# A conditioned four-stage residual kernel on one core: the first five periods from one written list, W1 laid out by 4p+c

## The chip, the cores and the metric

The kernel runs on one core of a Trainium2 chip. The metric is the device time of one execution in microseconds (us); lower is better. The engines are named as in the profile: PE (TensorE, matrix products; PEld its weight loads), DVE (VectorE), ACT (ScalarE), POOL (GpSimd) and SP (SyncE, which here only issues DMAs).

## What is computed

There are 128 samples x of 128 positions and 512 features. Four stages follow each other, each adding its result to x. The reference, cut to what matters:

```python
# stage 0, mask chosen by the sample's prompt type
s = einsum(tanh(x @ W0 + b0), v)                       # one score a position
p = softmax(where(mask[pt], s[:, None, :], -1e30))
x = x + (p @ x) / mask_count
# stage 1, weights chosen by the sample's language, 10 languages
a = relu(x @ W1[lang] + b1[lang]) @ W2[lang] + b2[lang]
x = x + layernorm(x + a) * gamma[lang] + beta[lang]
# stage 2, y = x as a 128 x 512 plane, reflecting edges
x = x + zX * lap_x(y) + zY * lap_y(y) + zR * y * (1 - y)
# stage 3, weights chosen by the sample's category, 64 categories
x = x + x @ W3[cat] + b3[cat]
```

W0 and W1[lang] are 512 x 128, W2[lang] is 128 x 512, W3[cat] is 512 x 512. All of it is float32.

## The kernel before

One sample is one tile: 128 positions on the partitions, 512 features along them. Stages 0 and 1 both begin with a product of x with a 512 x 128 matrix. These two products are taken together (`first_products`): x is turned so that features stand on the partitions, in four chunks of 128, and multiplied with W1[lang] and W0 side by side, held in `w10[b % 2]`. x + p @ x / count is then one product with p' = p / count + identity (`pooled`), and the adapter's second product is added to the same PSUM bank (`adapter`).

The order of all instructions is written out by hand. The list `plan` holds 46 parts, each with an offset: in period i the part (n, f) works on sample i + n. The stages of one sample so lie in different periods: first products for sample i + 1, pooling for i - 1, adapter for i - 2, the plane stage for i - 3 and the projection with W3 for i - 4. The main loop runs i from -2 to B + 4. The engines run their own instructions in that order and wait for each other by semaphores. Samples are loaded four periods ahead (`FIRST = 4`).

How x is turned. For samples 0 and 1 (`EARLY_X = 2`) `rejoin` turns x with four PE transposes and one ACT copy out of PSUM. For all others `halves` (an ACT copy, L247) splits the floats into two planes of 16-bit halves, `x_transpose` turns them with a transposing DMA on SP (L254), and `rejoin` (an ACT copy, L269) joins the halves.

Where W1 comes from. The table `w1_tab` holds W1 of all ten languages in SBUF, with b1 in one more column of each row (`W = D + 1`). `first_weights` copies the sample's row into `w10` (an ACT copy). For the first seven samples (`EARLY_W = 7`) `early_weights` loads W1[lang] straight from memory into `w10`, since the table is not there yet. Feature c*128 + p stands on partition p in chunk c; a chunk's rows are pieces of 512 bytes in memory.

What else the start must do. b2, gamma and beta of ten languages each (30 rows) have to be spread over all partitions. They are cut into three bfloat16 parts, and one PE product per row with a selecting column (`spread`, L230) writes the row into PSUM on all partitions; ACT or DVE copies it to its table (L233). The first four periods (`EARLY = 4`) run a changed copy of `plan` (`early_plan`), and the dictionary `once` hangs the spreading, the loading of `w1_tab` (`load_w1`, L118) and the factors of the plane stage onto parts of certain periods. `counts` (the number of allowed positions) and `neg_v` (-v) are made on DVE. b0 and v are broadcast by DMAs on ACT's queue, the ids, W2's table and the z factors come by SP.

Other lines that matter: L266 the PE transposes of x and L267 their copy (`rejoin`), L292 `first_products` (tile zh), L303 `hidden_bias`, L339 `scores` (sc), L369 and L374 `mix_transpose` and `mix_copy` (pTp, pT), L379 and L381 `pooled` (pool, h), L395 `with_beta` (POOL), L403 `adapter`, L426 `deviation` (POOL), L462 and L465 `y_transpose` (tr_y, tr_e), L471 to L473 `planes`, L515 `category` (the 1 MB of W3[cat]), L530 `residual` (POOL adds the identity to W3's diagonal, at steps of four floats), L537 `project` (po).

Of the kernel before, what the change touches and what calls it, by code (L numbers as in the profile page):

```python
# [10 lines left out]
I32 = mybir.dt.int32  # L11
# [12 lines left out]
def kernel(  # L24
# [46 lines left out]

    xt, w3t, b3t = {}, {}, {}
    FIRST = 4

    EARLY_X, EARLY_W = 2, 7
    W = D + 1
# [8 lines left out]
    def language(engine, b):  # L85
        return engine.snap(index(engine, 1, b, L - 1) * W)
# [4 lines left out]
    def early_weights(b):  # L91
        lang = index(nc.sync, 1, b, L - 1)
        nc.sync.dma_start(
            w10[b % 2][:, 0, :, :], w1[ds(lang, 1)].rearrange("o (c p) a -> p (o c) a", p=P)
        )

    ids = const.tile([1, 3, B], I32, name="ids")
    nc.sync.dma_start(ids[:, 1, :], lang_ids.unsqueeze(0))
    load_x(0)
    nc.sync.dma_start(w10[0][:, 1, :, :], w0.rearrange("(c p) a -> p c a", p=P))  # L100
    load_x(1)
    early_weights(0)
    early_weights(1)
    load_x(2)


    w1_tab = const.tile([P, L * W], F32, name="w1_tab")
    w2_tab = const.tile([A, L * W], F32, name="w2_tab")
    b2_tab = const.tile([P, L * W], F32, name="b2_tab")
    beta_tab = const.tile([P, L * W], F32, name="beta_tab")  # L110
    gamma_tab = const.tile([P, L * W], F32, name="gamma_tab")
# [4 lines left out]
    def load_w1(languages):  # L116
        for l in languages:
            nc.sync.dma_start(  # L118
                rows(w1_tab)[:, l, :D].rearrange("p (c a) -> p c a", c=NC),
                w1[l].rearrange("(c p) a -> p c a", p=P),  # L120
            )
# [14 lines left out]
    b0_sb = const.tile([P, A], F32, name="b0_sb")  # L136
    v_sb = const.tile([P, A], F32, name="v_sb")
# [7 lines left out]
    for dst, src in ((b0_sb, b0), (v_sb, v0)):  # L145
        nc.scalar.dma_start(dst, src.rearrange("a o -> (a o)").partition_broadcast(P))
    nc.sync.dma_start(ids[:, 0, :], pt_ids.unsqueeze(0))
    nc.sync.dma_start(ids[:, 2, :], cat_ids.unsqueeze(0))
    nc.sync.dma_start(rows(w2_tab)[:, :, :D], w2.rearrange("l a h -> a l h"))
    load_x(3)  # L150
    for dst, src in ((zx, z_x), (zy, z_y), (zr, z_r)):
        nc.sync.dma_start(dst, src.partition_broadcast(P))
    nc.sync.dma_start(rows(w1_tab)[:, :, D:W], b1t.unsqueeze(2))
# [3 lines left out]
    nc.gpsimd.tensor_copy(w10[1][:, 1, :, :], w10[0][:, 1, :, :])  # L157
# [20 lines left out]
    for i, (cmp, mult, step) in enumerate(  # L178
        ((ALU.is_ge, -1, 1), (ALU.is_ge, 1, -1), (ALU.not_equal, 1, -1))
    ):  # L180
        nc.gpsimd.affine_select(
            out=masks[:, i * P : (i + 1) * P],
            in_=masks[:, i * P : (i + 1) * P],
            compare_op=cmp,
            fill=BIG,
            base=0,
            pattern=[[step, P]],
            channel_multiplier=mult,
        )

# [9 lines left out]
    def counts():  # L200

        nc.vector.tensor_copy(row, row_i)
        nc.vector.tensor_scalar(d_pre, row, 1.0 - (S - 1), None, ALU.add)
        nc.vector.tensor_scalar(d_post, row, -1.0, 1.0, ALU.mult, ALU.add)
        nc.vector.tensor_copy(ptf, pt_i)
        nc.vector.tensor_scalar(cnt, ptf, 0.0, d_pre, ALU.is_equal, ALU.mult)
        nc.vector.tensor_scalar(sel, ptf, 1.0, d_post, ALU.is_equal, ALU.mult)
        nc.vector.tensor_add(cnt, cnt, sel)
        nc.vector.tensor_scalar_add(cnt, cnt, float(S - 1))

    counts()
    neg_v = const.tile([P, A], F32, name="neg_v")
    nc.vector.tensor_scalar_mul(neg_v, v_sb, -1.0)

    def factors():

        nc.vector.tensor_add(cy, zx, zy)
        nc.vector.tensor_scalar(cy, cy, -2.0, 1.0, ALU.mult, ALU.add)
        nc.vector.tensor_add(cy, cy, zr)
        nc.vector.tensor_scalar_mul(nzr, zr, -1.0)  # L220


    to_spread = [(t, i * L + l, l) for i, t in enumerate((b2_tab, gamma_tab, beta_tab)) for l in range(L)]

    def spread(n):
        for i in range(n):
            table, r, l = to_spread.pop(0)
            pool, tag = (ps_big, "big") if r % 3 else (ps_out, "po")
            ps = pool.tile([S, D], F32, tag=tag, name=f"row_{r}")
            nc.tensor.matmul(  # L230
                ps, pick[:, r : r + 1].to_broadcast([3 * G, P]), parts, start=True, stop=True
            )
            (nc.scalar.copy if r % 2 else nc.vector.tensor_copy)(rows(table)[:, l, :D], ps)  # L233
# [7 lines left out]
    def halves(b):  # L241
# [5 lines left out]
        nc.scalar.copy(s["split"], xt[b].bitcast(U16).rearrange("s (d i) -> s i d", i=2))  # L247
# [12 lines left out]
    def rejoin(b):  # L260
        s = st[b]
        s["xT"] = two.tile([P, NC, S], F32, tag="xT", name=f"xT_{b}")
        if b < EARLY_X:
            ps = ps_tr.tile([P, NC, S], F32, tag="tr", name=f"tr_x_{b}")
            for c in range(NC):
                nc.tensor.transpose(ps[:, c, :], xt[b][:, c * P : (c + 1) * P], ident)  # L266
# [7 lines left out]
    def act_index(b):  # L274
        st[b]["act_at"] = language(nc.scalar, b)

    def first_weights(b):
        if b < EARLY_W:
            if b > 1:
                early_weights(b)  # L280
            return
        nc.scalar.copy(
            w10[b % 2][:, 0, :, :].rearrange("p c a -> p (c a)"),
            w1_tab[:, ds(st[b]["act_at"], D)],
        )

    def first_products(b):
# [3 lines left out]
        for c in range(NC):  # L291
            nc.tensor.matmul(  # L292
                s["zh"],
                s["xT"][:, c, :],
                w10[b % 2][:, :, c, :],
                start=(c == 0),
                stop=(c == NC - 1),
            )
# [84 lines left out]
    def pooled_copy(b):  # L383
# [3 lines left out]
            s["h1"], s["h1p"], AF.Relu, bias=w1_tab[:, ds(s["act_at"] + D, 1)]  # L387
# [152 lines left out]

    def finish(b):
        nc.vector.tensor_add(b3t[b], st[b]["po"], b3t[b])

    def store(b):
# [20 lines left out]
        (-4, lambda b: project(b, [0])),  # L565
# [9 lines left out]
        (-4, lambda b: project(b, [1, 2])),  # L575
        (-1, pe_index),
        (-4, lambda b: project(b, [3])),
# [21 lines left out]

    EARLY = 4  # L600
    early_plan = list(plan)
    for part, place in (
        ((1, rejoin), (0, hidden)),
        ((1, first_products), (1, rejoin)),
        ((2, act_index), (-1, category)),
        ((2, first_weights), (2, act_index)),
    ):
        early_plan.remove(part)
        early_plan.insert(early_plan.index(place) + 1, part)
    once = {  # L610
        (-1, rejoin): [(spread, 8)],
        (0, first_products): [(spread, 3)],
        (0, masked): [(spread, 3)],
        (0, shares): [(spread, 3)],
        (1, first_products): [(spread, 3)],
        (1, masked): [(spread, 4)],
        (1, shares): [(spread, 6), (factors,)],
        (1, load_x): [(load_w1, range(0, 4))],
        (2, load_x): [(load_w1, range(4, 8))],
        (3, load_x): [(load_w1, range(8, L))],  # L620
    }
    for i in range(-2, B + 5):
# [43 lines left out]
```

## Time and profile before

| what | us |
|---|---|
| median of 3 runs | 1091.52 |
| lowest and highest | 1088.99 and 1091.77 |
| the profiled execution, its own time | 1090.35 |
| its span, first to last instruction | 1088.4 |
| PE busy | 1052.8 |
| DVE busy | 923.1 |
| ACT busy | 808.6 |
| POOL busy | 731.2 |

The profile is of one execution, so durations read from it are to be set against its own 1090.35 us. The granted PE clock over the span is 0.990 of full. A row of busy time by group gives line, engine, operation, tiles and shape, then how often, the total and the mean. The chain of waits follows the work that ended last back to its start. HBM delivered 209.13 MB and took 33.55 MB, together 223 GB/s over the span.

### The profile page before, as it was taken

The page shows a single profiled execution, that of the slowest core. Times are in us where ns is not written, and L with a number is a line of the kernel's source. Part 1 is how long each engine was busy: PE and PEld are TensorE (multiplying, and loading weights), DVE is VectorE, ACT ScalarE, POOL GpSimd, SP SyncE. Part 2 cuts the span into 40 slices and gives each one's busy share as a digit, 9 for nine tenths or more (in the row PEclk, how much of TensorE's full clock was granted, in tenths as well). Part 3 has the DMA queues.
Part 4 walks back from the last instruction along what each step waited for, and adds up shares of the span by engine and source line. Part 5 has one row for each costly group of instructions (what it writes and reads, how often), then busy time and mean ns, then how long its engine had stood idle before and what let it go on. Part 6 is the DMA issues. An engine that isn't in the chain of part 4 may idle for free.

```text
span 1088.4 us, 18571 instructions
## 1 busy us (share of the span) xinstructions
PE 1052.8 (97%) x3878; PEld 638.7 (59%) x3878; DVE 923.1 (85%) x2215; ACT 808.6 (74%) x1928; POOL 731.2 (67%) x780
## 2 busy tenths in 40 slices
PE   4689999999999999999999999999999999999997
PEld 2356566665666656666666566666665666656653
DVE  4568888888888888888888888888888888888886
ACT  3467877778778777787777777877777778777762
POOL 1156776767767667677676776776767767767675
PEclk9789999999999999999999999999999999999999
DMA  7699999999999999999999999999999999999973
GB/s 216 170 284 278 255 260 265 265 266 260 250 275 258 266 257 261 265 248 272 268 259 272 245 259 268 253 264 269 261 261 266 255 271 251 275 249 252 272 221 116
DMA packets 219920, 276.93 MB, mean 254 GB/s; under 512 B 142978, under 2 KB 152965, under 8 KB 203427
## 3 DMA queue, kind: packets, MB, share of 16 engines
q1 hardware_dynamic: 219318, 275.50, 97.5%
q8 instruction: 33, 0.54, 0.2%
q14 instruction: 77, 0.62, 0.2%
q10 hardware_dynamic: 492, 0.26, 0.1%
HBM read 209.13 MB, written 33.55 MB: 223 GB/s over the span
## 4 chain that ended last, share of the span: by engine, by line
PE 92%; DMA 3%; DVE 2%; ACT 2%; issue 1%; POOL 0%; DVEq 0%; ACTq 0%; SPq 0%; POOLq 0%
PE po L537 39%; PE zh L292 21%; PE pool L379 10%; PE pool L403 10%; PE tr_y L462 5%; PE tr_e L465 3%; PE h L381 2%; DMA turned<-split 2%; PE pTp L369 1%; PE sc L339 1%; PE row L230 1%; ACT split L247 1%; DMA v_sb<-in_L_cond_v_dram 1%; DMA w<-in_L_cond_W_dram 0%; DVE tr_y L497 0%
## 5 line engine op out<-in xcount | busy, mean ns | idle before, releaser
L537 PE MATMUL po<-w,x3T 128*128 128x512 f32 x1024 | 481.5, 593 | 1.3 <-issue 1.3
L292 PE MATMUL zh<-w,xT 128*128 128x256 f32 x1024 | 247.8, 386 | 9.2 <-ACT xT L269 8.2
L292 PEld LDWEIGHTS zh<-w,xT 128*128 128x128 f32 x1024 | 198.2, 194 | 92.5 <-ACT xT L269 40.8
L537 PEld LDWEIGHTS po<-w,x3T 128*128 128x128 f32 x1024 | 175.3, 191 | 125.8 <-issue 125.8
L426 POOL TENSOR_SCALAR ve<-mv 128x1 f32<-128x1 f32 x128 | 28.3, 221 | 294.9 <-DVE mv L423 294.9
L530 POOL TENSOR_TENSOR w<-w,ident 128x512 f32<-128x512 f32 x128 | 197.7, 1545 | 0.0
L307 ACT ACTIVATE zh<-zh 128x128 f32<-128x128 f32 x128 | 33.5, 262 | 194.8 <-DVE zh L303 194.8
L395 POOL TENSOR_TENSOR x<-x,beta_tab 128x512 f32<-128x512 f32 x128 | 152.5, 1191 | 36.9 <-ACT x L390 36.9
L269 ACT COPY xT<-turned 128x1024 uint16<-128x1024 uint16 x126 | 169.6, 1346 | 2.4 <-DMA turned<-split 2.4
L490 POOL TENSOR_TENSOR lr<-yT 128x512 f32<-128x512 f32 x128 | 163.6, 1278 | 0.0
L403 PE MATMUL pool<-w_tab,h1s 128*128 x256 | 132.1, 598 | 3.8 <-ACT x L390 3.8
L486 POOL TENSOR_TENSOR ud<-yT 128x512 f32<-128x512 f32 x128 | 133.0, 1039 | 1.5 <-ACT yT L473 1.5
L247 ACT COPY split<-x 128x1024 uint16<-128x1024 uint16 x126 | 132.1, 1048 | 1.9 <-DMA turned<-split 1.8
L379 PE MATMUL pool<-x,pT 128*128 128x512 f32 x256 | 131.8, 597 | 1.7 <-ACT pT L374 1.7
L462 PEld LDWEIGHTS tr_y<-ident,y 128*128 128x128 f32 x512 | 81.2, 204 | 64.6 <-issue 64.6
L303 DVE TENSOR_TENSOR zh<-zh,b_sb 128x128 f32<-128x128 f32 x128 | 38.3, 299 | 87.0 <-PE zh L292 85.6
L508 DVE SCALAR_TENSOR_TENSOR x3T<-lr,zx,tr_y 128x512 f32<-128x512 f32 x128 | 95.6, 747 | 14.5 <-DVE tr_y L501 1.7
L431 DVE SCALAR_TENSOR_TENSOR pool<-pool,mv,gamma_tab 128x512 f32<-128x512 f32 x128 | 97.1, 759 | 4.5
L478 ACT ACTIVATE own<-tr_y,cy,nzr 128x512 f32<-128x512 f32 x128 | 98.4, 769 | 0.0
L501 DVE SCALAR_TENSOR_TENSOR tr_y<-ud,zy,tr_y 128x512 f32<-128x512 f32 x128 | 95.5, 746 | 0.5 <-DVE q L364 0.2
L444 DVE SCALAR_TENSOR_TENSOR y<-pool,rstd,x 128x512 f32<-128x512 f32 x128 | 93.9, 733 | 0.4 <-POOL rstd L427 0.4
L418 DVE BATCH_NORM_STATS2 stats<-pool 128x6 f32<-128x512 f32 x128 | 89.5, 699 | 4.4
(79 smaller groups left out, 1616.8 us busy)
## 6 DMA issues: line engine op xcount, KB each, us to landing
w<-in_L_cond_W_dram SPq DMA_DIRECT2D x128, 1024.0 KB, 6.6
x<-in_x_dram SPq DMA_DIRECT2D x128, 256.0 KB, 4.5
b<-in_L_cond_b_dram SPq DMA_DIRECT2D x128, 256.0 KB, 4.6
out_dram<-b SPq DMA_DIRECT2D x128, 256.0 KB, 5.0
w_tab<-in_L_cond_W_dram SPq DMA_DIRECT2D x1, 2560.0 KB
w_tab<-in_L_cond_W_dram SPq DMA_DIRECT2D x10, 256.0 KB
w<-in_L_cond_W_dram SPq DMA_DIRECT2D x8, 256.0 KB, 4.4
turned<-split SPq DMA_TRANSPOSE x126, 4.9
```

The source lines that it names most:

```text
L247: nc.scalar.copy(s["split"], xt[b].bitcast(U16).rearrange("s (d i) -> s i d", i=2))
L269: nc.scalar.copy(s["xT"].rearrange("p c s -> p (c s)").bitcast(U16).rearrange("p (n i) -> p i n", i=2), s["turned"].rearrange("p i c s -> ...
L292: nc.tensor.matmul(s["zh"], s["xT"][:, c, :], w10[b % 2][:, :, c, :], start=(c == 0), stop=(c == NC - 1),)
L379: nc.tensor.matmul(s["xx"], s["pT"], xt[b], start=True, stop=True)
L395: nc.gpsimd.tensor_add(s["x1"], s["x1"], beta_tab[:, ds(at, D)])
L403: nc.tensor.matmul(s["xx"], s["h1"], w2_tab[:, ds(s["pe_at"], D)], start=False, stop=True, skip_group_check=True,)
L462: nc.tensor.transpose(s["yT"][:, c, :], yp[:, c + 1 : c + 2 + D - NC : NC], ident)
L478: nc.scalar.activation(s["own"], s["yT"], AF.Identity, bias=column(cy, b), scale=column(nzr, b))
L486: nc.gpsimd.tensor_add(s["ud"], planes[:, 1 : NC + 1, 0:S], planes[:, 1 : NC + 1, 2 : S + 2])
L490: nc.gpsimd.tensor_add(s["lr"], planes[:, 0:NC, 1 : S + 1], planes[:, 2 : NC + 2, 1 : S + 1])
L530: nc.gpsimd.tensor_add(diag, diag, ident.unsqueeze(1).to_broadcast([P, NC, P]))
L537: nc.tensor.matmul(s["po"], s["x3T"][:, c, :], w3t[b][:, c, :], start=(c == 0), stop=(c == NC - 1))
```

## The change

Six things are changed, all but the fourth in how the first periods are run.

1. Periods up to i = 4 no longer come from `early_plan` and `once`. One string, `ramp`, lists about 210 parts with their samples, and is run once in that order; the loop then starts at `START = 5` and leaves out what the list has done.
2. `EARLY_X` is 6: samples 0 to 5 are turned by PE transposes, and the split, the transposing DMA and the join begin with sample 6.
3. `EARLY_W` is 8. W1 of samples 0 to 5 is loaded into rows 0 to 5 of the table itself, which language l's own row later overwrites; samples 6 and 7 use `w10`. For samples 0 to 5 the first products are made in two halves, one with W0 from `w10[0]` and one with W1 from the table's row.
4. Feature 4p + c now stands on partition p in chunk c. W0 and W1 rows become one 2048-byte piece a partition; the PE transposes of x read every fourth float; and the split copy of all later samples reads its 16-bit elements at steps of 16 bytes.
5. b1 has a table of its own, [128, 10], and table rows are 512 floats instead of 513.
6. b0 and v are broadcast by SP's queue instead of ACT's. `counts`, `neg_v` and `factors` run on POOL instead of DVE. The list names for each of the 30 rows which engine copies it (`a` or `v`) and through which PSUM pool (`b`, `o`, `s`). W2's table comes in five loads of two languages instead of one of ten.

The diff, cut to its core:

```diff
-    EARLY_X, EARLY_W = 2, 7
-    W = D + 1
+    EARLY_X, EARLY_W, IN_TABLE = 6, 8, 6
 ...
     def early_weights(b):
         lang = index(nc.sync, 1, b, L - 1)
+        to = rows(w1_tab)[:, b, :] if b < IN_TABLE else flat(w10[b % 2][:, 0, :, :])
+        nc.sync.dma_start(to, w1[ds(lang, 1)].rearrange("o (p c) a -> p (o c a)", p=P))
+
+    def load_w1(l):
+        nc.sync.dma_start(rows(w1_tab)[:, l, :], w1[l].rearrange("(p c) a -> p (c a)", p=P))
+
+    def load_w2(l):
         nc.sync.dma_start(
-            w10[b % 2][:, 0, :, :], w1[ds(lang, 1)].rearrange("o (c p) a -> p (o c) a", p=P)
+            rows(w2_tab)[:, l : l + 2, :], w2[l : l + 2].rearrange("l a h -> a l h")
         )
 ...
-    nc.sync.dma_start(w10[0][:, 1, :, :], w0.rearrange("(c p) a -> p c a", p=P))
+    nc.sync.dma_start(w10[0][:, 1, :, :], w0.rearrange("(p c) a -> p c a", p=P))
+    for dst, src in ((b0_sb, b0), (v_sb, v0)):
+        nc.sync.dma_start(dst, src.rearrange("a o -> (a o)").partition_broadcast(P))
     load_x(1)
     early_weights(0)
     early_weights(1)
-    load_x(2)
 ...
+    def row_by(how, r):
+
+        table, l = (b2_tab, gamma_tab, beta_tab)[r // L], r % L
+        pool, tag = banks[how[1]]
+        ps = pool.tile([S, D], F32, tag=tag, name=f"row_{r}")
+        nc.tensor.matmul(
+            ps, pick[:, r : r + 1].to_broadcast([3 * G, P]), parts, start=True, stop=True
+        )
+        copies[how[0]](rows(table)[:, l, :], ps)
 ...
-        nc.scalar.copy(s["split"], xt[b].bitcast(U16).rearrange("s (d i) -> s i d", i=2))
+        nc.scalar.copy(
+            s["split"].rearrange("s i (c p) -> s i c p", c=NC),
+            xt[b].bitcast(U16).rearrange("s (p c i) -> s i c p", c=NC, i=2),
+        )
 ...
-                nc.tensor.transpose(ps[:, c, :], xt[b][:, c * P : (c + 1) * P], ident)
+                nc.tensor.transpose(ps[:, c, :], xt[b][:, c : c + D - NC + 1 : NC], ident)
 ...
-        for c in range(NC):
-            nc.tensor.matmul(
-                s["zh"],
-                s["xT"][:, c, :],
-                w10[b % 2][:, :, c, :],
-                start=(c == 0),
-                stop=(c == NC - 1),
-            )
+        if b < IN_TABLE:
+            w1_b = rows(w1_tab)[:, b, :].rearrange("p (c a) -> p c a", c=NC)
+            by = [(1, w10[0][:, 1, :, :]), (0, w1_b)]
+        else:
+            by = [(slice(0, 2), w10[b % 2].rearrange("p i c a -> p c i a"))]
+        for part, w in by:
+            for c in range(NC):
+                nc.tensor.matmul(
+                    s["zh"][:, part, :],
+                    s["xT"][:, c, :],
+                    w[:, c],
+                    start=(c == 0),
+                    stop=(c == NC - 1),
+                )
 ...
-            s["h1"], s["h1p"], AF.Relu, bias=w1_tab[:, ds(s["act_at"] + D, 1)]
+            s["h1"], s["h1p"], AF.Relu, bias=b1_sb[:, ds(s["act_lang"], 1)]
 ...
+    START = 5
+    ramp = """
+        load_x.2 pe_index.2 rejoin.0 act_index.0 pe_index.0 act_index.1 fetch_ids.2 act_index.2
+        pe_index.3 rejoin.1 act_index.3 act_index.5 first_products.0 act_index.4 fetch_ids.0
+        pe_index.1 early_weights.2 act_index.6 load_w2.0 copy_w0.0 load_w2.2 first_products.1
+        load_x.3 hidden_bias.0 row_at.2 early_weights.3 row_at.0 row_at.1 fetch_b1.0 hidden.0
+        row_by.ab.1 row_at.3 score.0 row_by.vb.0 row_by.ab.2 rejoin.2 row_by.vo.4 load_w2.4
+        row_by.vs.3 row_by.ab.5 load_w2.6 load_w2.8 mask_at.0 hidden_bias.1 category.0
 ...
+        category_row.1 shares.4 norm.2 edges.2 weights.4
+    """
+    done = set()
+    for part in ramp.split():
+        name, *how, number = part.split(".")
+        work = locals()[name]
+        work(*how, int(number))
+        done.add((work, int(number)))
+    for i in range(START, B + 5):
+        for number, work in plan:
+            if 0 <= i + number < B and (work, i + number) not in done:
                 work(i + number)
```

The loop's own order from sample 5 on, the PSUM pools and the buffers of x and W3 are as before.

## The prediction

> **What bounds the kernel now.** First view: the page's busy shares and slices.
>
> ```profile
> PE 1052.8 (97%) x3878; PEld 638.7 (59%) x3878; DVE 923.1 (85%) x2215; ACT 808.6 (74%) x1928; POOL 731.2 (67%) x780
> ...
> PE   4689999999999999999999999999999999999997
> ...
> PEclk9789999999999999999999999999999999999999
> ```
>
> TensorE (PE) is the bound, and only the first two or three slices of 27.2 us show it idle or slow. The chain of waits, in order of time, gives one full period afterwards; each row is start, duration, what.
>
> ```profile
> 71.77 1.73 PE zh L292 x8
> 73.50 0.86 PE pool L403 x2
> 74.36 0.47 PE tr_y L462 x4
> 74.83 0.24 PE tr_e L465 x2
> 75.07 0.11 PE pTp L369
> 75.18 0.86 PE po L537 x2
> 76.04 0.11 PE sc L339
> 76.15 0.86 PE pool L379 x2
> 77.01 0.22 PE h L381 x2
> 77.23 2.58 PE po L537 x6
> ```
>
> They sum to 8.04 us, and the next period's first products follow at 79.81: nothing is left between. 128 periods are 1029 of the 1088.4 us. The change leaves this loop's order as it is, so its place is the first 80 us. Next view: the same chain there, and the stretches by window (columns: window, length, PE busy, weight loads, DVE, ACT, POOL, granted clock, DMA share, GB/s).
>
> ```profile
> 5.29 5.75 DMA v_sb<-in_L_cond_v_dram
> ...
> 26.51 1.23 ACT xT L269
> ...
> 46.69 7.57 DMA turned<-split
> ```
>
> ```profile
> 0.00:15.97 15.97, 6.56 (x17) 3.55 (x18) 8.15 (x24) 4.42 (x7) 3.59 (x12) 1.00 0.74 235
> ...
> 26.21:33.03 6.82, 5.24 (x12) 3.26 (x13) 0.57 (x1) 2.22 (x5) 0.00 (x0) 0.50 0.56 193
> ...
> 39.86:46.69 6.83, 4.68 (x8) 2.24 (x8) 4.13 (x12) 4.00 (x7) 1.28 (x1) 0.50 0.53 136
> ...
> 53.52:60.34 6.82, 4.68 (x14) 3.86 (x15) 0.97 (x2) 2.23 (x2) 0.00 (x0) 0.50 1.11 333
> ...
> 0.00:79.65 79.65, 51.94 (x160) 28.93 (x160) 43.72 (x116) 38.23 (x84) 22.48 (x33) 0.87 0.83 223
> ```
>
> The reader is to see the 5.75 us wait for the broadcast v, the 7.57 us wait for a transposing DMA of x, and three stretches at half clock. The first stretch was at half clock too, though its column says 1.00: the row matmuls at 11.94 took 2.38 us for five, two at 20.41 took 0.45. No engine but PE is near full: ACT 38, DVE 44 of 79.65 us.
>
> **The sum before.** I compare one place that both programs reach with the same work ahead of it: the start of the first products of sample 6, at 79.65 us now. Warm PE work ahead of it, with the chain's durations: six first products 6 x 1.73 = 10.4; five pooled 5 x 1.08 = 5.4; four adapters 3.4; three y transposes 3 x 0.71 = 2.1; eleven small transposes 1.2; two projections 2 x 3.44 = 6.9; 30 rows x 0.225 = 6.8; two x transposes 0.9. Together 37.1. Half of the busy time in the four cold stretches is surcharge: (6.56 + 5.24 + 4.68 + 4.68) / 2 = 10.6. The rest, 79.65 - 37.1 - 10.6 = 31.9, is PE idle with hand-off latencies.
>
> **The change, part by part.**
>
> *x of samples 2 to 5 by TensorE.* Adds 16 transposes: 4 x 0.47 (row tr_y) = +1.9 us of PE. Removes four split copies (L247, 1.05), four rejoin copies (L269, 1.35) and adds four plain copies (L267, 0.59): -7.2 us of ACT. Removes four transposing DMAs from SP (1.43 issue, 4.9 to landing) and their waits for ACT, behind which w3 and W1 loads stood: in the first 90 us SP stood 8.4 us before one of them waiting for a copy on ACT, 5.3 before another.
>
> *First products in two halves.* Eight more weight loads a sample would matter if they did not overlap; L381 streams 128 columns in two passes in 0.22, so eight chunk halves are 1.76 against 1.73. Six samples: +0.2 us.
>
> *W1 of eight samples from memory.* Eight loads instead of seven; six land in the table's rows and are overwritten later, so sample b's load no longer waits for the products of b-2. SP issues 42 copies and 13 indexed ones up to w3 of sample 3, at 0.42 and about 0.8 more for the index (4.06 to 4.82 in the trace): 28 us of a 60 us stretch, not the bound. The later table loads do wait for products on SP, and queued behind the longest of these waits (about 36 to 41 us) are x_8, w3 of sample 3 and x_6's transposing DMA, and the first of them to be needed is x_6, at the rejoin copy near 53. The 1280 four-byte pieces of b1 become 128 pieces; SP loses about 2 us of DMA at 18 to 21 us.
>
> *Features 4p+c.* W rows become 2 KB in one piece. x's PE transposes read every fourth float, as tr_y already does. The split copy in the loop (122 left) now reads 2-byte elements 16 bytes apart. No row shows that on ACT. Below: no gain, since today's 1.048 us for 1024 elements is 0.83 ns each plus 0.2 fixed (L471: 0.60 for 512). Nearest rows: tr_y reads one float per 16 bytes at 0.47 / 4 / 128 = 0.92 ns, like the contiguous pTp (0.11); L530 on POOL, 16-byte steps in and out, takes 1.545 against 1.191 for L395, so 1.30 x. **A rule against the change:** the Trainium skill, "SBUF — State Buffer", Door 1, says the memory has 16-byte lines and wants at least two hits per line, each crossing being penalised. The new read has one hit per line, though the page's widest free step for 16-bit elements, 8, is just this step: it sits at the rule's edge. I put the upper end at twice, 2.1 us. Slack: pTp is done, and ACT takes pT up at 203.87, just as split ends at 203.97; pT is copied at 204.14 and PE wants it at 204.59. So 0.45 us is hidden. By the PE row (my value) it costs 0, by the POOL row +0.31, hidden; by the rule taken at twice, (1.05 - 0.45) x 122 = +73 us.
>
> *Broadcasts and small work.* b0 and v move from ACT's queue to SP, ahead of x_1 and W1: v's landing (11.03 now) should come near 7, x_1's (6.0 now) near 7. Thirteen small operations go from DVE to POOL, bounded by L426 (0.22) and L395 (1.19); at about 0.35 each they end near 12 us, before sample 0's shares near 20. POOL was idle for 34.8 us there, which hides them at either end up to 0.6 each. Seven index reads on ACT (about 0.8 each) stand early, between the first x copies: 5 us, of which the wait for W1 covers most.
>
> *The list.* Rows are strewn between products instead of eight at 9 us. Going down the five queues in their order with the durations above: x_0's transposes at 4.1 as now, x_1's after another 2.2 us idle, products of samples 0 and 1 without a break from about 8 to 15 us. That fills a 3.4 us stretch (12.55 to 15.97 did so before, after which the clock rose), so the clock rises near 12.6 and the surcharge is about 4.0. Later every 6.8 us stretch is over 70% busy in this walk. Before, a drop came after stretches with 3.84, 4.39 and 3.60 us busy of 6.83 (one with 4.14 passed). Rows leave gaps of 0.1 to 0.9 us waiting for one of 19 ACT copies (0.59) or 11 DVE copies (0.69): about 5. The y transposes of samples 0 and 2 and the adapter of 2 wait about 1 us each: 3. DMA: the 14.5 MB up to w3 of sample 3 take 41 us at 353 GB/s (10 to 17 us now), and that w3 is used near 60.
>
> **Sum after.** Work 37.1 + 1.9 + 0.2 = 39.2; surcharge 4.0; idle 4.1 + 2.2 + 5 + 3 = 14.3; together 57.5 instead of 79.65: -22.1. The span goes from 1088.4 to about 1066.3; the profiled execution took 1090.35, so about 1068.3. The median of the runs shown, 1091.52, is 1.2 higher: I say **1069**. With idle at its least (the first 6.3 alone) it is -30; with only the named waits gone (4.0 and 4.2 ahead of zh, 5.3 ahead of the rows) idle is 18.4 and cold surcharge perhaps 8, -14.
>
> **Rivals.**
>
> *A. Main, 0.73:* as summed; own range 1063 to 1076.
>
> *B. The ramp stays ragged, 0.13.* Each row still goes PE, copy, PE, and the broadcasts ahead of x_1 and W1 may land as slowly as v did (5.75 us after issue), +3; two stretches that fall cold add 2 x 2.3; hand-offs double, +5. Together 12 of the 22 are lost: about 1081. For it: the L230 rows waited 8.2 us before. Against it: most of that was start-up.
>
> *C. Slower, 0.10: ACT's split becomes the limit.* Beyond 0.45 us of extra, each further 0.1 us costs 12 us. At 0.45 + 22 / 122 = 0.63 extra (a split of 1.68 us) the gain is gone; at 2.1 the result is 1069 + 73 = 1142. For it the rule, against it the PE row.
>
> *D. Nothing, 0.04.* The period's first products would be held by something else, a landing of w3 or x for instance: 1089 to 1093. At 79.65 the loop is PE-bound with all engines below 93%, so little speaks for it.
>
> A difference of 0.3%, 3.3 us, is about what a measurement can tell. From the cases: faster 0.86 (A and B), same 0.03, slower 0.11 (C and a little of D). The range 1061 to 1081 takes in A and most of B.
>
> **What would show it.** First products of sample 6 at 55 to 60 us; no transposing DMA in the chain before 45 us; the clock up by 13 us and steady; 30 row copies spread to about 35 us; PE idle before zh falling from 9.2. The split's mean: at 1.05 the loop is unchanged at 8.04 us, above 1.5 case C holds and pool waits for pT on PE. Wrong if the ramp ends before 80 us but the period is longer, or if PE waits for W1 or x landings after 20 us.

## The result, and the profile after

The changed kernel takes 1155.1 us (median of four runs, 1153.95 to 1157.86) against 1091.47 us for the kernel before (four runs, 1088.99 to 1091.77). The ratio is 1.0592, with a 95% interval of 1.0567 to 1.0617: **5.9% slower**, where 1069 us and a gain were forecast. The profiled execution took 1153.95 us with a span of 1152.2.

The first 80 us did what was forecast of them, and every period after them became longer. From the page of the kernel after: busy time of PE, its 40 slices, the granted clock, the shares of the chain that ended last, and two groups (total and mean ns of one, then idle time before it and what ended that).

```profile
PE 1076.9 (93%) x3942; PEld 638.2 (55%) x3942; DVE 929.3 (81%) x2198; ACT 915.5 (79%) x1927; POOL 752.8 (65%) x793
...
PE   7899999999999999999999999999999999999997
...
PEclk9999999999999999999999999999999999999999
...
PE 63%; ACT 27%; DVE 5%; issue 3%; DMA 1%; DVEq 0%; SPq 0%; POOL 0%; POOLq 0%
...
L256 ACT COPY split<-x 128x1024 uint16<-128x1024 uint16 x122 | 252.0, 2065 | 0.4 <-DMA turned<-split 0.3
...
L392 PE MATMUL pool<-x,pT 128*128 128x512 f32 x256 | 143.5, 642 | 56.9 <-ACT pT L387 56.8
```

The same two groups in the kernel before:

```profile
L247 ACT COPY split<-x 128x1024 uint16<-128x1024 uint16 x126 | 132.1, 1048 | 1.9 <-DMA turned<-split 1.8
L379 PE MATMUL pool<-x,pT 128*128 128x512 f32 x256 | 131.8, 597 | 1.7 <-ACT pT L374 1.7
```

The slices look healthy, and the clock row shows 9 throughout. A digit 9 means 90% or more, so it does not tell 93% from 97%. The other rows do. ACT now holds 27% of the chain. The split copy takes 2.065 us instead of 1.048. PE stands 56.8 us in front of the pooled products, waiting for ACT's copy of pT; before, that was 1.7 us.

The ramp, in stretches by window of the kernel after (window; length, PE busy, weight loads, DVE, ACT, POOL, granted clock, DMA share, GB/s):

```profile
0.00:9.58 9.58, 4.00 (x18) 3.65 (x19) 4.04 (x11) 2.66 (x4) 3.68 (x16) 1.00 0.66 190
...
0.00:57.06 57.06, 45.04 (x224) 29.18 (x224) 38.45 (x99) 35.35 (x84) 27.91 (x46) 1.00 0.96 300
```

The first products of sample 6 start at 57.06 us instead of 79.65; 57.5 was forecast. The clock is reported full from 9.58 us on, and no half-clock stretch follows within the span. The 1.00 of the first row is not to be trusted: four transposes of x took 1.10 us at 4.05 and 0.63 us at 13.38.

One period of the kernel after, in the chain of waits in order of time (start, duration, what):

```profile
302.81 1.74 PE zh L305 x8
...
304.58 0.31 DVE zh L316
...
304.91 0.27 ACT zh L320
...
305.21 0.02 ACT z L322
...
305.37 2.07 ACT split L256
307.44 0.17 ACT pT L387
...
307.65 1.13 PE pool L392 x2
308.78 0.22 PE h L394 x2
309.00 2.58 PE po L550 x6
311.57 1.74 PE zh L305 x8
```

Before, this chain held PE alone. Now it leaves PE after the first products, goes through DVE's bias and ACT's activation, stands 2.07 us in the split copy, and comes back to PE through pT. From one zh to the next it is 8.76 us, a ring through three engines; the PE work of a period is 8.04 us, as before. (Periods are given below as the median distance between the first products of neighbouring samples, from 200 to 1000 us: 8.761 us here, 8.037 before.) From 57.06 to the end of the span are 1095.1 us, before from 79.65 to the end 1008.8: 86.4 us more, or about 119 times the 0.724 us by which a period is longer. The ramp's gain of 22.6 us is set against this, and 86.4 - 22.6 = 63.8 us is the loss.

The wait row holds only some 55 of these 86 us, for two reasons. A wait of PE is counted from the modelled end of the matmul before it, here that of sc, which is put at 0.27 us, though in the kernel before the next products start 0.11 us after it: 122 times 0.16, or 20 us. And the pooled products themselves take 642 ns instead of 597: 256 times 45 ns, or 12 us.

### The profile page after: what moved, and what is told of

Its sections match the earlier page's. It is cut to its first block, busy times and chain, and to the rows that moved or that the text cites. A ratio compares the mean times of both kernels' runs of the same rounds, so it can differ in the third digit from the quotient of the medians.

```text
span 1152.2 us, 18686 instructions
## 1 busy us (share of the span) xinstructions
PE 1076.9 (93%) x3942; PEld 638.2 (55%) x3942; DVE 929.3 (81%) x2198; ACT 915.5 (79%) x1927; POOL 752.8 (65%) x793
## 4 chain that ended last, share of the span: by engine, by line
PE 63%; ACT 27%; DVE 5%; issue 3%; DMA 1%; DVEq 0%; SPq 0%; POOL 0%; POOLq 0%
PE po L550 28%; ACT split L256 22%; PE zh L305 19%; PE pool L392 12%; DVE zh L316 3%; ACT zh L320 3%; PE h L394 2%; ACT pT L387 2%; DMA turned<-split 1%; PE row L239 0%; PE pool L416 0%; ACT z L322 0%; DMA x<-in_x_dram 0%; PE tr_x L278 0%; PE tr_y L475 0%
## 5 line engine op out<-in xcount | busy, mean ns | idle before, releaser
L256 ACT COPY split<-x 128x1024 uint16<-128x1024 uint16 x122 | 252.0, 2065 | 0.4 <-DMA turned<-split 0.3
L305 PE MATMUL zh<-w,xT 128*128 128x256 f32 (+1 forms) x1024 | 237.8, 375 | 0.0
L305 PEld LDWEIGHTS zh<-w,xT 128*128 128x128 f32 x1024 | 192.5, 191 | 77.4 <-ACT xT L281 29.2
L408 POOL TENSOR_TENSOR x<-x,beta_tab 128x512 f32<-128x512 f32 x128 | 162.9, 1273 | 78.9 <-ACT x L403 61.7
L392 PE MATMUL pool<-x,pT 128*128 128x512 f32 x256 | 143.5, 642 | 56.9 <-ACT pT L387 56.8
L281 ACT COPY xT<-turned 128x1024 uint16<-128x1024 uint16 x122 | 164.4, 1347 | 0.0
L392 PEld LDWEIGHTS pool<-x,pT 128*128 128x128 f32 x256 | 38.4, 188 | 126.4 <-ACT pT L387 124.9
```

What stands on the lines that cost most here:

```text
L256: nc.scalar.copy(s["split"].rearrange("s i (c p) -> s i c p", c=NC), xt[b].bitcast(U16).rearrange("s (p c i) -> s i c p", c=NC, i=2),)
L281: nc.scalar.copy(s["xT"].rearrange("p c s -> p (c s)").bitcast(U16).rearrange("p (n i) -> p i n", i=2), s["turned"].rearrange("p i c s -> ...
L305: nc.tensor.matmul(s["zh"][:, part, :], s["xT"][:, c, :], w[:, c], start=(c == 0), stop=(c == NC - 1),)
L392: nc.tensor.matmul(s["xx"], s["pT"], xt[b], start=True, stop=True)
L408: nc.gpsimd.tensor_add(s["x1"], s["x1"], beta_tab[:, ds(at, D)])
```

## The experiments

The theory (S): the split's doubled duration, and nothing else of the change, makes the loop longer, because it stands on ACT ahead of pT. Its rivals: the loss lies in another part of the list or of the layout (weight reads, PE's strided reads, the two-half products); or (Q) it lies in the order of ACT's queue, and moving the split mends it. About the copy itself there were three theories: the two hits in a 16-byte line that the Trainium skill asks for ("SBUF — State Buffer", Door 1); a price for a step of 8 elements, whatever their size in bytes (W); a price for the loop nest of the copy (N).

**All of the change but the layout: list_old_layout.**

```diff
-    ... "(p c) a -> p c a" for W0 and W1; xt[b][:, c : c + D - NC + 1 : NC] for the transposes
-        nc.scalar.copy(
-            s["split"].rearrange("s i (c p) -> s i c p", c=NC),
-            xt[b].bitcast(U16).rearrange("s (p c i) -> s i c p", c=NC, i=2),
-        )
+    ... "(c p) a -> p c a" for W0 and W1; xt[b][:, c * P : (c + 1) * P] for the transposes
+        nc.scalar.copy(s["split"], xt[b].bitcast(U16).rearrange("s (d i) -> s i d", i=2))
```

> The changed kernel with features laid out as before (c*128+p on partition p): W0 and W1 rows again in 512-byte pieces, the PE transposes of x unstrided, and the split copy reading at steps of 4 bytes. The list, TensorE for six samples and W1 of eight samples stay. Theory S (the split copy's 16-byte steps alone make the loop longer): split back to 1.05 us, period back to 8.04 us, first products of sample 6 near 57 us, in all 22 us below the kernel before: 1066 to 1072 us. Rival L (the loop is longer because of how the list hands over to it, or because of the table's new row length): the period stays near 8.76 and the time near 1155. Rival H (half and half: the layout's 2 KB pieces also carry the ramp's gain): period 8.04, but first products of sample 6 later than 62 us, 1074 to 1082 us.

Measured: 1070.95 us (1068.57 to 1071.95), ratio 0.9825 (0.9803 to 0.9846). Groups of this kernel:

```profile
L393 PE MATMUL pool<-x,pT 128*128 128x512 f32 x256 | 131.8, 597 | 1.2 <-ACT pT L388 1.0
L260 ACT COPY split<-x 128x1024 uint16<-128x1024 uint16 x122 | 127.9, 1048 | 3.8 <-DMA turned<-split 3.7
```

The split is 1.048 us again, the wait for pT is gone, the period is 8.038 us, and sample 6 starts at 57.33. So the list with all its other parts is worth 1.8%, and the layout is the whole loss.

**The layout alone: layout_alone.** The kernel before, with only the features moved to 4p + c.

```diff
-    "(c p) a -> p c a"                      # W0, W1
+    "(p c) a -> p c a"
-    nc.tensor.transpose(ps[:, c, :], xt[b][:, c * P : (c + 1) * P], ident)
+    nc.tensor.transpose(ps[:, c, :], xt[b][:, c : c + D - NC + 1 : NC], ident)
     ... and the split of the kernel after
```

> The kernel before with the layout 4p+c alone: W0, W1 in 2 KB pieces, PE transposes of x at every fourth float, the split copy of 126 samples at steps of 16 bytes; everything else as before. Theory S: split 2.07 us, period 8.76 us, so 126 x 0.72 = 91 us longer less what the start hides: 1172 to 1185 us. Rival L: the period stays 8.04, 1086 to 1093 us.

Measured: 1181.03 us (1179.88 to 1182.18), ratio 1.0831 (1.0801 to 1.0862). Its groups:

```profile
L247 ACT COPY split<-x 128x1024 uint16<-128x1024 uint16 x126 | 260.0, 2064 | 0.1
...
L382 PE MATMUL pool<-x,pT 128*128 128x512 f32 x256 | 144.9, 648 | 58.5 <-ACT pT L377 58.4
```

The split and the wait are those of the kernel after, at a period of 8.763 us, without any of the list. The two parts nearly add up: 1091.5 + 90.3 (this one's loss over its own comparison, 1090.7) - 19.8 (the list's gain) = 1162, against 1155.1 measured. Of the 7 us between, 3.6 are in the ramp of layout_alone, whose samples 2 to 5 go through the slow split too: its sample 6 starts at 83.28 us instead of 79.65. The rest was not traced.

**What the copy pays for: copy_steps.** Six rounds of plain copies of 1024 elements a partition, at various steps. It computes nothing of the reference; its output is x.

```diff
+        nc.scalar.copy(au, u[:, 0 : 1*N : 1])      # L71 uint16, read step 2 B
 ...
+        nc.scalar.copy(au, u[:, 0 : 4*N : 4])      # L73 uint16, read step 8 B
+        nc.scalar.copy(au, u[:, 0 : 8*N : 8])      # L74 uint16, read step 16 B
 ...
+        nc.scalar.copy(af, big[:, 0 : 4*N : 4])    # L78 float32, read step 16 B
 ...
+        nc.scalar.copy(..., x4)                    # L80 the split of the kernel after
+        nc.scalar.copy(...)                        # L81 its elements with c innermost: step 4 B
+        nc.scalar.copy(..., x8)                    # L82 both halves of a float, then 16 B on
+        nc.scalar.copy(wu[:, 0 : 2*N : 2], u[:, 0:N])  # L83 write step 4 B
 ...
+        nc.scalar.copy(wu[:, 0 : 8*N : 8], u[:, 0:N])  # L85 write step 16 B
 ...
```

> Copies alone, measured by themselves: 1024 elements a partition on ACT, DVE and POOL, read at growing steps, six of each; the output is a plain copy of x, nothing of the reference is computed. Rule theory (16-byte lines, two reads a line are needed): ACT on 16-bit elements takes about 1.05 us at steps of 2, 4 and 8 bytes and about 2.07 at 16 and 32; floats take 1.05 at 4 and 8 bytes and 2.07 at 16 and 32. Rival W (what costs is a step of 8 elements, not of bytes): floats at 16 bytes (4 elements) take 1.05. Rival N (what costs is the loop nest of three dimensions in the copy): the plain 16-byte step takes 1.05 and only the split's own pattern 2.07. Writing 16-bit elements at steps takes 1.35, as the join copy does.

Measured, in the groups of this kernel on ACT (mean ns behind the total; the means of L71, L73 and L82 each hold one longer copy of 1.34 to 1.37 us, their medians are 1.044, 1.094 and 1.087):

```profile
L85 ACT COPY act_wide<-big 128x1024 uint16<-128x1024 uint16 x6 | 28.4, 4725 | 0.0
...
L74 ACT COPY act_u<-big 128x1024 uint16<-128x1024 uint16 x6 | 12.0, 2003 | 0.0
L78 ACT COPY act_f<-big 128x1024 f32<-128x1024 f32 x6 | 12.0, 1996 | 0.9 <-DMA big<-in_x_dram 0.9
L80 ACT COPY act_u<-big 128x1024 uint16<-128x1024 uint16 x6 | 11.9, 1987 | 0.0
L83 ACT COPY act_wide<-big 128x1024 uint16<-128x1024 uint16 x6 | 8.0, 1328 | 0.0
L73 ACT COPY act_u<-big 128x1024 uint16<-128x1024 uint16 x6 | 6.9, 1147 | 0.0
L82 ACT COPY act_u<-big 128x1024 uint16<-128x1024 uint16 x6 | 6.8, 1138 | 0.0
...
L71 ACT COPY act_u<-big 128x1024 uint16<-128x1024 uint16 x6 | 6.6, 1098 | 1.6 <-DMA big<-in_x_dram 1.5
L81 ACT COPY act_u<-big 128x1024 uint16<-128x1024 uint16 x6 | 6.3, 1048 | 0.0
```

The column to read is the mean. Floats and 2-byte elements at 16-byte steps cost the same 2.0 us (L78, L74), though 16 bytes are 4 of the ones and 8 of the others: it is the step in bytes, so W falls. The plain 16-byte step, which has no nest, costs as much as the split of the kernel after (L74 and L80, 2.00 and 1.99), and a nest that reads the two halves of a float together costs 1.14 (L82): it is not the nest, so N falls. In L82 every second read goes on to another 16 bytes, and it is cheap all the same, for two reads fall in each. One hit a line is what costs on ACT. There the page's sentence on two hits held; its figure for the widest free step, 8 elements of 16 bits or 4 floats, is one doubling too far: here 8 bytes cost 1.05 times a contiguous read, and 16 bytes 1.9 times. Writes are another matter: 1.33 us at 4 bytes, 4.73 at 16.

**Only ACT's time, or the strided read itself: split_twice.** The old layout with the cheap split made twice.

```diff
+        nc.scalar.copy(s["split"], xt[b].bitcast(U16).rearrange("s (d i) -> s i d", i=2))
```

> The list with the old layout (1070.95 us), and the split copy of the loop made twice, one straight after the other into the same tile: ACT is held for about 2.0 us at the same place, by reads at steps of 4 bytes. Theory T (only the time for which ACT stands in front of pT counts): 0.96 us more than the plain split, 0.05 less than the 16-byte read costs, so a period of 8.70 us and 1071 + 122 x 0.66 = 1146 to 1154 us. Rival M (the strided read disturbs others at the memory as well, PE or POOL): less than 8.5 us, below 1130 us.

Measured: 1163.49 us (1161.79 to 1165.46), ratio 1.0674 (1.0656 to 1.0692), period 8.821 us. Its groups:

```profile
L394 PE MATMUL pool<-x,pT 128*128 128x512 f32 x256 | 143.4, 642 | 63.9 <-ACT pT L389 63.9
L261 ACT COPY split<-x 128x1024 uint16<-128x1024 uint16 x122 | 127.5, 1045 | 3.9
L260 ACT COPY split<-x 128x1024 uint16<-128x1024 uint16 x122 | 127.9, 1048 | 0.4 <-DMA turned<-split 0.3
```

No read here has a wide step, and the same wait of PE for pT is back. So the time for which ACT is held is enough to make the loss. It came out some 10 us above the upper end expected: the second copy holds ACT for 1.08 us more (2.03 instead of 0.95), not 0.96, and the ramp is 2.4 us longer, with the clock at half from 20.6 to 24.0 us (sample 6 starts at 59.76). The hidden 0.30 us, on which that expectation rested, was taken from the kernel after; the next run tests it with a smaller copy.

**How much is hidden: split_and_384.** The old layout, with a second copy of 384 elements behind the split.

```diff
         nc.scalar.copy(s["split"], xt[b].bitcast(U16).rearrange("s (d i) -> s i d", i=2))
+        nc.scalar.copy(s["split"][:, 0, 0:384], xt[b].bitcast(U16)[:, 0:768:2])
```

> The list with the old layout, and after each split of the loop a copy of 384 of its elements once more: ACT is held about 0.42 us longer in front of pT. If 0.45 us are hidden, as the prediction read from the trace: period 8.04 us, 1069 to 1074 us. If 0.30 are hidden, as the 16-byte split (1.02 us more, period 0.72 longer) says: period 8.16, 1071 + 122 x 0.12 = 1083 to 1090 us.

Measured: 1102.28 us (1100.88 to 1103.85), ratio 1.01 (1.0078 to 1.0121). From its timeline (start, duration, engine, what):

```profile
303.28 1.05 ACT L260 COPY split<-x 128x1024 uint16<-128x1024 uint16 x1
304.36 0.51 ACT L261 COPY split<-x 128x384 uint16<-128x384 uint16 x1
304.78 0.26 ACT L389 COPY pT<-pTp 128x128 f32<-128x128 f32 x1
...
305.09 1.12 PE L394 MATMUL pool<-x,pT 128*128 128x512 f32 x2
306.06 0.39 PE L396 MATMUL h<-pT,z 128*128 128x128 f32 x2
```

From the start of the split to that of pT's copy are 1.50 us, 0.55 more than with the split alone, and the period is 8.287 us, 0.25 more: 0.30 us are hidden, not 0.45. The time lies above both ranges expected, since the small copy holds ACT for more than the 0.42 us reckoned with and the ramp is 2.9 us longer (sample 6 starts at 60.26, with the clock at half from 20.2 to 27.1); the period decides between them. The table puts the kernels of one order side by side (hold: from the start of the split to the start of pT's copy).

| kernel | hold us | more than 0.948 | period us | more than 8.038 |
|---|---|---|---|---|
| list_old_layout | 0.948 | 0 | 8.038 | 0 |
| split_and_384 | 1.498 | 0.55 | 8.287 | 0.25 |
| after | 1.964 | 1.02 | 8.761 | 0.72 |
| split_twice | 2.032 | 1.08 | 8.821 | 0.78 |

Each row loses its extra hold less 0.30 us. Where the rest of the 0.45 went can be read beside the kernel before, where pT ended at 204.14:

```profile
204.49 0.30 PEld L379 LDWEIGHTS pool<-x,pT 128*128 128x128 f32 x2 [0.29 <-ACT pT L374]
204.59 1.02 PE L379 MATMUL pool<-x,pT 128*128 128x512 f32 x2
...
205.45 0.27 PE L381 MATMUL h<-pT,z 128*128 128x128 f32 x1
```

and the kernel after, where PE waits for pT:

```profile
307.65 0.30 PEld L392 LDWEIGHTS pool<-x,pT 128*128 128x128 f32 x2 [1.02 <-ACT pT L387]
307.65 1.13 PE L392 MATMUL pool<-x,pT 128*128 128x512 f32 x2 [0.46 <-ACT pT L387]
```

Before, the load of pT as weights starts 0.10 us ahead of the products; after, both start at once, and the products take 0.96 us to the start of the next ones instead of 0.86 (in split_and_384, above, 0.97). That is 0.10 of the 0.45. Another 0.05 is the hand-off: the products start 0.05 us after the end of pT's copy at the soonest.

**The split elsewhere in ACT's order: split_after_planes and split_before_hidden.** Both keep the layout of the kernel after and move `halves` and `x_transpose` of sample i + 2: behind pT, or ahead of the first products' bias and activation.

```diff
-        (2, halves), (2, x_transpose),   # before (0, masked)
+        (2, halves), (2, x_transpose),   # split_after_planes: after (-3, planes)
+        (2, halves), (2, x_transpose),   # split_before_hidden: before (0, hidden_bias)
```

> The changed kernel with the split copy and the transposing DMA of the loop moved on ACT's and SP's queues behind the copies pT and planes (one place in the plan, loop only). The split stays 2.07 us. Theory S in its narrow form (the cost is that the split stands in front of pT, for which PE waits): PE no longer waits for pT; ACT is busy about 7.2 of 8.04 us a period, so the period falls to 8.04 to 8.3 and the time to 1068 to 1100 us. Rival Q (ACT's ring as a whole is too long: what the split pushes back is exps, xT and the copy of x, each of which PE or DVE wait for): the wait moves to zh's xT or to exps, period 8.5 to 8.8, 1125 to 1160 us.

> The changed kernel, the 16-byte split kept at 2.07 us, but put (with its transposing DMA) in front of hidden_bias in the loop's list, where ACT idles about 1.5 us a period waiting for DVE. Ring theory (the loop is as long as the ring zh - hidden - split - pT - pooled - po - zh): the split starts about 1.5 us earlier, delays hidden by about 0.6 us, which delays the score and sc, which PE wants about 0.75 us later than it gets it; pT no longer waits. Period 8.04 to 8.25, 1068 to 1097 us. Rival Q (wherever it stands, the lengthened ACT queue makes something late, as behind planes, where xT came 0.93 us late): period 8.5 or more, over 1125 us.

Measured: split_after_planes 1212.03 us (1209.22 to 1212.13), ratio 1.1107 (1.1081 to 1.1133), period 9.224; split_before_hidden 1118.28 us (1117.61 to 1119.89), ratio 1.0257 (1.024 to 1.0274), period 8.442. From the waits of split_after_planes between 200 and 1000 us (who waited for whom: us in total, times, longest):

```profile
PEld zh L305 <- ACT xT L281: 152.6, 87, 2.0
...
PE zh L305 <- ACT xT L281: 80.6, 87, 1.2
```

Behind pT, the copy no longer holds pT, but the xT that the next first products need is queued behind it: PE waits 0.93 us a period (80.6 / 87) there, and the kernel is slower still, beyond what even Q gave. The wait moved where Q had it; the narrow form of S is wrong. In split_before_hidden three waits share the loss: in the same stretch ACT waits 99.7 us for DVE's `least`, the loads of PE 77.9 us for `masked` and 72.4 us for xT. It came out between what the two theories gave and does not separate them. The place matters, then: ahead of the bias the copy costs 28 us against the kernel before instead of 64, behind pT 121. But in none of the three places tried does nobody wait for a copy of 2 us; other places were not tried.

**A layout with both: pair_layout.** Feature 256k + 2p + j on partition p: two neighbouring floats stay together, so the split reads at 8-byte steps, and a row of W comes in two pieces of 1 KB.

```diff
+        nc.scalar.copy(
+            s["split"].rearrange("s i (k j p) -> s i k j p", k=2, j=2),
+            xt[b].bitcast(U16).rearrange("s (k p j i) -> s i k j p", k=2, j=2, i=2),
+        )
-    "(p c) a -> p c a"
+    "(k p j) a -> p k (j a)"
-    xt[b][:, c : c + D - NC + 1 : NC]
+    xt[b][:, c // 2 * 2 * P + c % 2 : (c // 2 + 1) * 2 * P : 2]
```

> The changed kernel with features k*256 + 2p + j on partition p in chunk 2k + j: W rows come in pieces of 1 KB, PE transposes of x read every second float, the split copy reads at steps of 8 bytes in four dimensions (two elements of a pass per 16-byte line). The rest as changed. Theory S (two reads a line are free): split 1.09 to 1.12 us as the 8-byte copy measured alone, under the 0.3 us that are hidden, period 8.04 us, 1067 to 1073 us. If the four dimensions cost by themselves: split above 1.3 us, and more than 1080 us.

Measured: 1068.73 us (1067.08 to 1069.6), ratio 0.9807 (0.9791 to 0.9824). Its split, from its groups:

```profile
L265 ACT COPY split<-x 128x1024 uint16<-128x1024 uint16 x122 | 140.4, 1151 | 2.5 <-DMA turned<-split 2.4
```

At 1.15 us, a little above the 1.09 to 1.12 expected, the split holds ACT 0.10 us longer than the old one, inside the hidden 0.30, and the period is 8.037 us. This version beats both kernels; from list_old_layout, whose interval overlaps, it cannot be told apart. Its sample 6 starts at 55.78 us.

**Where the ramp's gain comes from.** The step on x by TensorE was tried alone, and taken out of the list.

```diff
-    EARLY_X, EARLY_W = 2, 7
+    EARLY_X, EARLY_W = 6, 7              # x6_alone, on the kernel before
     # x6_b1_table: and b1 in a table of its own
     # x6_b1_small: and b0, v by SP, and neg_v, counts, factors on POOL
-    EARLY_X, EARLY_W, IN_TABLE = 6, 8, 6
+    EARLY_X, EARLY_W, IN_TABLE = 2, 8, 6   # list_dma_turned, on list_old_layout,
     # halves and x_transpose of samples 2 to 5 put into the list ahead of each rejoin
```

> The kernel before with x of six samples instead of two turned by PE; its own order of the first periods, layout and W1 loads kept. The prediction put the transposing DMAs of samples 2 to 5 down as two of the named waits (4.0 and 4.2 us ahead of zh), with 7.2 us less of ACT. If they carry the ramp: first products of sample 6 near 67 us instead of 79.65, 1075 to 1083 us. If the order of the list carries it: less than 5 us, 1086 to 1092 us.

> The list with the old layout (1070.95 us), but x of samples 2 to 5 turned by split, transposing DMA and join as before; the splits and DMAs stand in the list some 8 us ahead of each join. If TensorE for six samples is needed for the gain: first products of sample 6 later by more than 8 us (four splits and joins add 7.2 us to ACT, and SP stands before each transposing DMA), 1079 to 1090 us. If the list can hide them: within 3 us of 1071.

> The kernel before with x of six samples by PE and b1 in a table of its own; its order of the first periods kept. In the trace with six samples by PE alone, 6.54 us of the chain are a wait of ACT's h1s (L386) for a load of the W1 table, because b1 stands in that table, and SP's loads in turn waited for h1s. If that wait took the place of the ones removed: 6 to 12 us below 1091, 1079 to 1085 us. If not: within 4 us of 1091.

> As x6_b1_table, and b0 and v by SP's queue ahead of x_1, neg_v, counts and factors on POOL; still the old order. The chain held 5.75 us for v, in front of the row copies on DVE. Those gone, PE's rows and the first products of sample 0 start about 2 to 3 us earlier: 2 to 6 us below x6_b1_table. What then remains to 1071 us belongs to the list's order and to W1 from memory for more samples.

Sample 6 is read from one profile of each; the ratios are against the runs of the kernel before made beside each, with medians of 1090.4 to 1090.8 us.

| kernel | sample 6 starts, us | time, us | ratio, 95% |
|---|---|---|---|
| before | 79.65 | 1091.47 | |
| x6_alone | 78.26 | 1091.18 | 0.9993 to 1.0029 |
| x6_b1_table | 76.29 | 1089.44 | 0.9976 to 1.001 |
| x6_b1_small | 77.00 | 1087.78 | 0.9955 to 0.9984 |
| list_dma_turned | 71.04 | 1082.53 | 0.9883 to 0.9938 |
| list_old_layout | 57.33 | 1070.95 | 0.9803 to 0.9846 |

On the kernel before, six x by TensorE gain nothing. Its chain has this in their place:

```profile
52.19 6.54 DMA w_tab<-in_L_cond_W_dram
```

The activation h1s takes its bias from the W1 table, and here it is released by the landing of a row of W1 in that table. But with b1 in its own table the time is 1089.44 us, where 1079 to 1085 would have shown that wait to be the cause. ACT's own line tells why:

```profile
58.84 0.37 ACT L386 ACTIVATE h1s<-h,w_tab 128x128 f32<-128x128 f32 x1 [0.29 <-DMA w_tab<-in_L_cond_W_dram]
```

ACT had other copies to do until shortly before and stood idle for 0.29 us. The 6.54 us are the flight of the DMA, which the chain follows back from the last to arrive; they are not time that its absence would give back (sample 6 came 2.0 us sooner, in one profile of each). With b0, v and the small work moved too, x6_b1_small lies 1.7 us below x6_b1_table, where 2 to 6 were expected; their intervals overlap.

Within the list, TensorE's turning is worth 13.7 us of ramp (71.04 to 57.33). In list_dma_turned SP stood up to 6.6 us before a transposing DMA, waiting for ACT, and the clock was at half twice (18.3 to 25.1 and 38.7 to 49.0 us). The DMAs were tried in one place of the list each, so a better one is not excluded. The rest, some 17 us between x6_b1_small and list_old_layout, belongs to the written order together with W1 of eight samples and the other parts of the list; it was not taken apart further.

## Why the prediction was wrong

**The step that failed** is the cost of the split at 16-byte reads. The prediction put the extra at 0 by the PE row ("my value"), at 0.31 by the POOL row, and at twice, 2.1 us in all, as the upper end. The copy takes 2.065 us: the upper end, nearly. The nearest row was chosen by the pattern of addresses, and it belonged to another engine. It also showed only half of what PE does. PE's weight loads have rows of their own (PEld), and there the step is seen. The loads of the x transposes at full clock, with reads at steps of 16 bytes (after) and contiguous (list_old_layout):

```profile
L278 PEld LDWEIGHTS tr_x<-ident,x x16: 195/203/217, 13.2 to 33.4; 128*128 128x128 f32 x16
...
L279 PEld LDWEIGHTS tr_x<-ident,x x16: 138/140/144, 14.6 to 34.6; 128*128 128x128 f32 x16
```

and the two rows that the prediction compared, y at steps and q contiguous, in the kernel before:

```profile
L462 PEld LDWEIGHTS tr_y<-ident,y 128*128 128x128 f32 x512 | 81.2, 204 | 64.6 <-issue 64.6
...
L369 PEld LDWEIGHTS pTp<-ident,q 128*128 128x128 f32 x128 | 19.8, 154 | 0.8 <-PE row L230 0.8
```

So the step does cost PE, 203 ns a load instead of 140. Most of it does not show, because loads overlap the products: four transposes of x take 0.47 us instead of 0.44. On ACT the whole price stands in the copy's time. So the trace of before already held a warning, in PE's weight loads. POOL's row misled too: it compared two different operations (1.30), while plain copies on POOL in copy_steps, with DVE's running beside them, have medians of 1.124 us contiguous and 2.759 at 16-byte steps, 2.5 times. No row of ACT at this step existed, and what the Trainium skill says of two hits a line ("SBUF — State Buffer", Door 1) was the only evidence that spoke of the memory rather than of another engine; the page's widest free step was given too much weight against it. So case C should not have had 0.10.

**Case C's mechanism was right, its size was 13 us short.** It gave 1142 us, and "pool waits for pT on PE" is what the trace shows. The term that was mis-sized is the hidden part: 0.30 us, not the 0.45 between pT's end and its use. That is 0.15 x 119 = 18 us. An extra of 1.02 instead of 1.05 takes back 4, and the time without the slow split was 1071 instead of 1069; together 1142 + 18 - 4 + 2 = 1158, against 1155.1. The point from which it decides was not 0.63 us of extra but about 0.30 + 22.6 / 119 = 0.49.

**The ramp, by its own steps.**

- Its sum was right: 57.06 against 57.5 us for sample 6, a gain of 22.6 against 22.1. That it came so near is in part luck, for two errors inside it cancel. The surcharge is half of the 4.00 us of PE busy before 9.58, so about 2.0 instead of 4.0, because the clock rose at 9.58 and not near 12.6: the prediction waited for a full stretch of 3.4 us, and here the 3.41 us ahead of the rise held 2.89 us of PE work. Idle, taken as what the forecast work leaves over, is then 57.06 - 39.2 - 2.0 = 15.9 instead of 14.3. Sample 0's products start at 7.58 us, near the 8 forecast.
- Main case A was, except for the layout, the kernel list_old_layout: 1070.95 us against 1069, inside its own range of 1063 to 1076. Case B's drops of the clock did not come in the kernel after; they came in list_dma_turned.
- The longer pieces of W1 bought little: 57.06 with the 2 KB pieces against 57.33 with the old layout. Some of their gain may be hidden, since the slow split of the first loop samples stands twice in the ramp's chain of the kernel after (from 39.03 and from 51.15 us). The most that a layout brought is the 1.5 us of pair_layout, and a single profile of each does not make that sure. The layout thus paid 86 us in the loop for a third of a microsecond, or at most these 1.5, in the ramp.
- TensorE's transposes were credited with the ACT and SP time that they free. On the kernel before they bring nothing (x6_alone). They need the written order to become time.

**The signs named there served.** The split's mean above 1.5 us and pool waiting for pT are the two rows that settled the reading, and "the ramp ends before 80 us but the period is longer" is what happened. The signs for the ramp came true: no transposing DMA in its chain before 45 us, the last row copies near 32 us, and no idle time of PE before zh, where it was 9.2 us.

## What to carry to other kernels

When a change alters the access pattern of an instruction inside the loop, price it by a row of the same engine with the same step; if there is none, time the copy by itself, as copy_steps did in one run. The other engines' rows are no bound, and the cost of being wrong is the difference times the number of periods. An engine at 74% of the span can still be the next bound: what counts is which of its copies stands in the ring between two products, and how long it may be held before PE notices (here 0.30 us). If data must be laid out in wide steps for a one-time gain, look for a layout that keeps two neighbours together: the pair layout kept the gain at a tenth of a microsecond a period, hidden.

## What the runs showed of the hardware

- ACT's copy of 1024 elements a partition takes, by the median in copy_steps, 1.04 us at read steps of 2 and 4 bytes, 1.09 at 8, 1.98 at 16 and 2.02 at 32; floats at 4, 8, 16 and 32 bytes take 1.04, 1.11, 1.98 and 2.02. The price comes where each read falls in another 16 bytes, and hardly grows beyond that. Two 2-byte reads in the same 16 bytes and then 16 on take 1.09.
- ACT's writes are dearer and do not level off: 1.32 us at a step of 4 bytes, 2.45 at 8, 4.71 at 16.
- PE's weight loads pay for steps as well: 0.140 us contiguous, 0.206 at steps of 8 bytes (pair_layout, medians of 16) and 0.203 at 16. Eight bytes, nearly free on ACT, cost PE as much as 16; why stays open. Little of it reaches the time of the transposes, 0.47 us for four instead of 0.44.
- Pooled products that PE had to wait for took 0.96 to 0.97 us to the next products instead of 0.86; their weights were not loaded ahead.
